# One fp32 transformer block on one core: the FFN's own DVE and ScalarE work entered in the scheduler's clock, six places for weight tiles in two sizes, and Wk loaded in four column chunks

## The chip, the cores and the metric

The kernel runs on one core of one Trainium2 chip. The metric is device time in microseconds, from a launch to its end. Before the change the median of three runs is 1770.16 us (1769.39 to 1774.62).

## What is computed

Everything is fp32: x is (4, 2048, 512), the context (4, 128, 512). Cut to what matters:

```python
# attention, per batch b: one head, 128 keys
xn = layernorm(x)
attn = softmax((xn @ Wq + bq) @ (ctx @ Wk + bk).T) / sqrt(512)
x1 = x + tanh(g_xattn) * (attn @ (ctx @ Wv + bv))
# FFN, one of 8 experts chosen per batch from the mean over the sequence
z = layernorm(x1)
e = argmax(z.mean(axis=1) @ Wr + br)
out = x1 + tanh(g_ffn) * (relu(z @ W1[e] + b1[e]) @ W2[e] + b2[e])   # 512 -> 2048 -> 512
```

## The kernel before

**The FFN** does nearly all the work. Per batch there are two pairs of blocks (a block is 512 rows) and two halves of the hidden width: 4 x 2 x 2 = 16 passes, called stage 0 to 15 below. Both layers are multiplied by Strassen's scheme in the Winograd form, which trades multiplications for sums. Layer 1 uses it twice, one inside the other: 7 groups (`ORDER`) of 7 products (`inner`), so 49 products of two matmuls. The matmuls of all products are recorded at one line, L798 (`chain`), with the names X, Y and Q for the PSUM banks; `z,w` are layer 1, `w,h` and `w,s` layer 2. The last three products of a group (5, 4, 3) run within the next group's. Layer 2 uses the scheme once: 7 products, each in two halves of eight matmuls (a pair below). ScalarE copies a bank to start the next (L817, L1032, L1043, L1064) and applies relu (L962); DVE and GpSimd do the sums (L978 to L1058, L1119, `hsum` L921).

**Weights.** The sums of weights that the scheme needs are made on the chip once per batch and half, mostly by GpSimd (`stage_half`): base blocks are loaded (L588, L594), summed (L559), and stored to a DRAM buffer, W1d or W2d (L580). Each pass then loads its tiles from there (L777, L771), or from W2 directly where no sum is needed (L764). `items` lists these loads in the order of use: for a group of layer 1 a left tile "A" (4 of 7 products, 4 KB per partition) and a right tile "B" (the last three, 3 KB in a place of 4 KB), for layer 2 seven tiles "2" (4 KB). `NW = 5` places take them in that order. After each group, and after each second half in layer 2, `fetch` issues as many loads as places have come free. The two loads of y, the running output of 1 MB each (L941, `sums_load`), are issued after group 5 in the first half of each pair, ahead of that group's `fetch`.

**Attention** for batch 0 runs ahead of the FFN. For batches 1 to 3 it runs inside the FFN: a generator per block (`attention`) that yields after each step what engines it used and for how long. Its steps: load x (L199, on ScalarE's queue) and xT (L201, on SP's), statistics on DVE (L208) and `pow` on GpSimd (L214), scores on TensorE (psc, L228) and DVE (L235), exp on ScalarE (L247), transposes (pp, L256), their copy (L259), the product with V (four pav, L282), which DVE adds into x (L270), statistics again, the store x1d (L293), normalising on ScalarE (L297), 16 transposes (pt, L329) that ScalarE copies back into x's buffer (L316), and the store z2d (L337) from there. pav and pt use two PSUM banks in turn, so a third waits until the first is read. There is one buffer for x, which the next block's load must wait for. The DMA semaphores are eight and used in turn, so every DMA also waits until the eighth before it in the program has landed.

**The order** is set in Python, as the program is written, by a clock that counts microseconds of TensorE: `tick` advances it after each product of layer 1 and each half of eight matmuls in layer 2. A stream (attention is `slow`, the weight sums are `staged`) may take its next step when the time `at` that its former steps have been given is at most `SOON` ahead of the clock, and when its pace allows: `PACE` times the clock's advance is the number of steps it may take. `free` holds when an engine is next free. Inside the FFN only GpSimd is kept there: steps on DVE and ScalarE add their time, times a factor of 1.3, to the stream's own `at`, and the FFN's own instructions add nothing but for a few on GpSimd (`pool_takes`). Each engine executes its own instructions strictly in the order written, and SP its DMAs.

**The set-up** loads the context of batch 0 (ctxT0), Wk in two column halves and Wq, makes keys (pk, L412) on TensorE, centres Wq on DVE (L463 to L465), and multiplies the two (pm, L412). ctxT0 and the keys KT0 lie in the two places of the pool `wk`, which the scores of attention use later.

Of the kernel before, what the change touches and what calls it, by code (L numbers as in the profile page):

```python
# [18 lines left out]
P = 128  # L19
# [70 lines left out]
def flamingo(tc, ctx, x, xT, cxT, g_x, g_f, WqT, Wk, Wv, bqk, bv, Wr, br, W1, b1, W2, b2, out):  # L90
# [4 lines left out]
    KC, FC = H // P, FF // P  # L95
    NW = 5
    TB = 4 * P
# [61 lines left out]

    zsum, Zs = {}, {}  # L160
    MV = {}
    done_at, clock = {}, {"now": 0.0}
# [30 lines left out]
    def attention(b, blk, pools):  # L193


        (xp, tag_x), (xTp, tag_xT), wk, ps_t, ps_a, queue = pools

        xt = xp.tile([P, 4, H], F32, tag=tag_x, name=f"x_{b}_{blk}")
        queue.dma_start(xt, rows(x, b, blk))  # L199
# [4 lines left out]
        def statistics():  # L204
            mv = small.tile([P, 4, 2], F32, tag="mv", name="mv", bufs=4)
            for t in range(4):
                st = small.tile([P, 6], F32, tag="st", name="st", bufs=4)
                nc.vector.bn_stats(st, xt[:, t, :])  # L208
                nc.vector.bn_aggr(mv[:, t, :], st)
                yield (("DVE", 0.85),)  # L210
            rstd = small.tile([P, 4], F32, tag="rstd", name="rstd", bufs=4)
            ve = small.tile([P, 4], F32, tag="ve", name="ve", bufs=4)
            nc.vector.tensor_scalar(ve, mv[:, :, 1], EPS, None, ALU.add)  # L213
            nc.gpsimd.tensor_tensor(rstd, ve, mhalf, ALU.pow)  # L214
            yield ("DVE", 0.15), ("POOL", 1.05), ("POW", 0.0 if ahead_of_ffn[0] else 1.0)
            return mv, rstd
# [29 lines left out]
        for t in range(4):  # L246
            nc.scalar.activation(  # L247
                sc[:, t, :], sc[:, t, :], AF.Exp,
                bias=nmax[:, t : t + 1], accum_out=ssum[:, t : t + 1],
            )  # L250
            if t % 2:
                yield (("ACT", 1.2),)
        yield from room(ps_t)
# [9 lines left out]
        nc.vector.tensor_scalar(coef, coef, gx, None, ALU.mult)  # L263
        yield (("ACT", 0.6),), (("DVE", 0.4),)
        while MV[b][1] is None:
# [76 lines left out]
    mvp = pool("mvp", 1)  # L342
    xp, xTp, wkp = pool("xp", 1), pool("xTp", 1), places("wk", 2)
    ps_t, ps_a = places("ps_t", 1, space=PSUM), places("ps_a", 1, space=PSUM)
# [17 lines left out]

    def in_home(p, tag, *shapes):

        t = p.tile([P, 4 * H], F32, tag=tag, name="home")
        at, out = 0, []
        for shape in shapes:
            n = int(np.prod(shape))
            v = t[:, at : at + n]
            names = "abcd"[: len(shape)]  # L370
            out.append(
                v.rearrange(
                    f"p ({' '.join(names)}) -> p {' '.join(names)}", **dict(zip(names, shape))
                ) if len(shape) > 1 else v
            )
            at += n
        return out

    if True:
        M0 = mvp.tile([P, KC, S], F32, tag="M", name="M_0")  # L380
        V0 = mvp.tile([P, H], F32, tag="V", name="V_0")
        ctxT0 = wkp.tile([P, 1, KC, S], F32, tag="wk", name="ctxT0")
        ctxTr = sp.tile([P, B - 1, KC, S], F32, name="ctxTr")
        w = {name: sp.tile([P, KC, H], F32, name=f"w{name}") for name in ("k", "q", "v")}
        bvb = sp.tile([P, H], F32, name="bvb")
        KT0 = wkp.tile([P, KC, S], F32, tag="wk", name="KT0")
        KTr, V3 = in_home(hp, "s2", (KC, (B - 1) * S), (H,))
# [6 lines left out]
        nc.sync.dma_start(ctxT0, cxT[:, 0:1])  # L394
        for c in range(2):
            nc.sync.dma_start(w["k"][:, :, c * Q : (c + 1) * Q], Wk[:, :, c * Q : (c + 1) * Q])
        with nc.allow_non_contiguous_dma(reason="bias"):
# [343 lines left out]
    items = [i for i in items if i[0] or i[1] == "2" or i[2] >= HERE]  # L741
    ring = {"issued": 0, "freed": 0}

    def ring_tile(kind):
        t = wp.tile([P, 4 * Q], F32, tag="w", name="w")
        if kind == "2":
            return t.rearrange("p (k c) -> p k c", k=4)
        k = 4 if kind == "A" else 3
        return t[:, 0 : 2 * k * P].rearrange("p (c k f) -> p c k f", c=2, k=k)

    def fetch(freed=0):

        ring["freed"] += freed
        while ring["issued"] < min(ring["freed"] + NW, len(items)):
            st, kind, i = items[ring["issued"]]
            b, fh = st // (2 * NF), st % 2
            need = (b, fh, "2" if kind == "2" else RIGHT[ORDER[i]])
            if need not in made and not (kind == "2" and RIGHT[ORDER2[i]] < 3):
                return
            t = ring_tile(kind)  # L760
            if kind == "2":
                m = ORDER2[i]
                if RIGHT[m] < 3:
                    nc.sync.dma_start(  # L764
                        t.rearrange("p (a k) c -> p a k c", a=2),
                        W2[bass.ds(expert[b][0], 1), fh, :, :, RIGHT[m]].rearrange(
                            "e a p k c -> p (e a) k c"
                        ),
                    )
# [38 lines left out]
    def inner(product, copied, begun, summed, done):  # L808
# [4 lines left out]
        def m1():  # L813
            t["X"] = bank("X")
            product(t["X"], 1, True)
            t["Y"] = bank("Y")
            nc.scalar.copy(t["Y"], t["X"])  # L817

        def m7():
# [27 lines left out]

    def pool_takes(us):
        free["POOL"] = max(free["POOL"], clock["now"]) + us

# [66 lines left out]
    def hsum(to, a, b, op, cp):  # L917

        for k in (slice(0, 2), slice(2, 4)):
            x, y, z = (t[:, cp, k, :] for t in (to, a, b))  # L920
            nc.vector.tensor_tensor(x, y, z, op)  # L921

    def s3(cp):
# [19 lines left out]
    def ffn1(b, blk, fh):  # L943
# [10 lines left out]
        def relu(ij, j, src):  # L954
# [6 lines left out]
            for c in range(2):  # L961
                nc.scalar.activation(  # L962
                    h[ij][:, v, 2 * m + c, :], src[:, c, :], AF.Relu,
                    bias=b1T[:, f + c : f + c + 1],
                )

        def ctile():
# [5 lines left out]
        def sums(m, j, v, eng):  # L973

            if m in BASE:
                ij, base = BASE[m]
# [17 lines left out]
        def group(i):  # L994
# [35 lines left out]
            def copied(v):  # L1030
                t = s7p.tile([P, 2, Q], F32, tag="s7", name="s7")
                nc.scalar.copy(t, v)  # L1032
                if m not in BASE:
                    return {21: t, 22: t}
# [3 lines left out]

            def begun(q, y):
                if m in BASE:  # L1040
                    nc.vector.tensor_tensor(q, BASE[m][1][21], y, ALU.add)
# [6 lines left out]

            def summed(j, a, v):
                if m == 1:  # L1050
                    nc.vector.tensor_tensor(first(j), a, v, ALU.add)
# [4 lines left out]
                else:  # L1056
                    c = cp_.tile([P, 2, Q], F32, tag="cg", name="cg", bufs=3)
                    nc.vector.tensor_tensor(c, a, v, ALU.add)  # L1058
                    sums(m, j, c, nc.gpsimd)
                    pool_takes(1.3)  # L1060

# [9 lines left out]
        for i in range(8):  # L1071
# [14 lines left out]
            left = 0 if s else HERE  # L1086
            fetch((cur is not None and i >= left) + (last is not None and i > left))
            if i == left:
# [5 lines left out]
    def ffn2(b, blk, fh, half):  # L1094
# [21 lines left out]
        def add(cp, j, v):  # L1116
            i, m = divmod(j - 11, 10)
            o = Ys[i][:, 2 * cp : 2 * cp + 2, m * Q : (m + 1) * Q]
            nc.vector.scalar_tensor_tensor(o, v, gf, o, ALU.mult, ALU.add)  # L1119

        def group(cp):
# [59 lines left out]

    BUSY = {"PE": 1.0, "DVE": 1.3, "ACT": 1.3, "POOL": 1.0, "DMA": 1.1, "Q": 1.1, "POW": 4.0}

    class Stream:
# [3 lines left out]
        def step(self):  # L1188
# [9 lines left out]
            elif chains:  # L1198
                ends = []
                for chain_ in (chains,) if isinstance(chains[0][0], str) else chains:  # L1200
                    t = self.at
                    for engine, us in chain_:
                        if engine == "POOL":
                            t = free[engine] = max(free[engine], t) + us
# [42 lines left out]
    while True:  # L1247
        s_ = min(parts, key=lambda s: s.at)
        if filler and max(filler.at, free["PE"]) + (SLACK if (0, NBLK - 1) not in done_at else PRESS) <= s_.at:
            if not filler.step():  # L1250
                filler = None
                setup.close()
                wp = pool("wp", NW, side="right")
            continue
# [44 lines left out]
    due = {"slow": 0.0, "staged": 0.0}  # L1299
    PACE = {"slow": (1.0,.9,.9), "staged": (3.,3.,3.,3.)}  # L1300
    next_stage = 1
    SOON = 0.8

    def paced(name, stream, more):

        due[name] = min(due[name] + more, 1.0 + more)
        while stream and due[name] >= 1 and stream.at <= clock["now"] + SOON:
            due[name] -= 1
# [4 lines left out]
    def tick(dt, weight):  # L1313
# [5 lines left out]
        for s_ in list(loose):  # L1319
            while s_.at <= clock["now"] + SOON:  # L1320
                if not s_.step():
# [8 lines left out]
    for b in range(B):  # L1330
        for blk in range(NF):
            for fh in range(2):
# [11 lines left out]
                for _ in ffn2(b, blk, fh, lambda: tick(1.73, 1.25)):  # L1344
                    for _ in range(3):
                        for name, us in next(prep, None) or ():
                            if name == "POOL":
                                pool_takes(us)
                    tick(1.73, 1.25)
# [33 lines left out]
```

## Time and profile before

| | |
|---|---|
| median of 3 runs | 1770.16 us |
| the profiled execution | 1770.84 us, span 1769.1 us |
| TensorE busy / weight loads | 1687.6 us (95%) / 1440.1 us (81%) |
| DVE, ScalarE, GpSimd busy | 1042.5, 581.4, 656.8 us |
| mean granted TensorE clock | 0.988 |
| DMA | 381.88 MB, 216 GB/s mean |
| FFN from, last matmul ends | 116 us, 1764.6 us |

The span goes from the first to the last instruction. Lines of groups read: line, engine, operation, what it writes and reads; waits read: who waited, for whom, us in total, times, longest. In a timeline a line is start, duration, and in brackets the idle time before it with the instruction that ended it; SPq and ACTq are the DMAs issued from SP and ScalarE. In the windows each line is a stretch with the busy time of each engine, the granted clock (1.00 is full speed), the DMA engines' busy share and GB/s.

### The profile page before, as it was taken

How to read it: one execution, taken by the hardware profiler on the slowest of the kernel's cores; microseconds unless marked ns; L12 is line 12 of the kernel's file. 1: busy time of each engine (PE TensorE's matmuls, PEld its weight loads, DVE VectorE, ACT ScalarE, POOL GpSimd, SP SyncE). 2: the span in 40 equal slices, each digit the busy share in tenths (PEclk: the TensorE clock that was granted, in tenths of full speed). 3: DMA queues.
4: the chain of work that ended last, by engine and by line, in shares of the span. 5: the costliest groups of instructions: out<-in, count | busy, mean ns of one | idle time of the engine just before them, and what ended most of it. 6: DMA issues, size and time to landing. Idle time of an engine off the chain costs nothing.

```text
span 1769.1 us, 21983 instructions
## 1 busy us (share of the span) xinstructions
PE 1687.6 (95%) x7966; PEld 1440.1 (81%) x7966; DVE 1042.5 (59%) x1663; ACT 581.4 (33%) x1284; POOL 656.8 (37%) x536
## 2 busy tenths in 40 slices
PE   6888988989999989899999999999999999999998
PEld 5667867877888878788887888888888888888887
DVE  5756837537578547566756666484546463656362
ACT  1514224143241432424334152332324141415150
POOL 0464513410069541244614940168644410251010
PEclk9999999999999999999999999999999999999999
DMA  7277767373678784638787693487767452535241
GB/s 292 96 265 301 256 236 249 104 265 104 217 276 331 266 335 163 228 119 299 263 301 246 252 353 139 153 290 245 250 246 282 140 185 87 184 125 200 78 142 70
DMA packets 142012, 381.88 MB, mean 216 GB/s; under 512 B 10448, under 2 KB 39120, under 8 KB 127568
## 3 DMA queue, kind: packets, MB, share of 16 engines
q1 hardware_dynamic: 135856, 342.43, 55.5%
q10 hardware_dynamic: 6048, 38.04, 5.5%
q8 instruction: 64, 1.05, 0.2%
q14 instruction: 44, 0.36, 0.1%
HBM read 262.99 MB, written 117.44 MB: 215 GB/s over the span
## 4 chain that ended last, share of the span: by engine, by line
PE 81%; DMA 8%; DVE 6%; POOL 2%; ACT 2%; issue 1%; SPq 0%; ACTq 0%; DVEq 0%; POOLq 0%
PE Y L798 32%; PE Q L798 21%; PE X L798 20%; PE psc L228 3%; DMA w<-W1d 2%; PE pav L282 2%; DMA z2d<-x 2%; DVE st L208 1%; DMA W1d<-base 1%; PE pt L329 1%; DMA w<-in_W_dram 1%; POOL home L559 1%; DMA base<-in_W_dram 1%; DVE x L270 1%; DVE c L990 1%
## 5 line engine op out<-in xcount | busy, mean ns | idle before, releaser
L798 PE MATMUL Y<-z,w 128*128 128x256 f32 x1296 | 325.0, 384 | 23.8 <-DMA w<-W1d 6.6
L798 PEld LDWEIGHTS Y<-z,w 128*128 128x128 f32 x1296 | 243.4, 191 | 73.4 <-issue 11.3
L962 ACT ACTIVATE h<-c,b1T 128x256 f32<-128x256 f32 x512 | 229.1, 501 | 91.0 <-DVE c L978 33.5
L559 POOL TENSOR_TENSOR base<-base 128x512 f32<-128x512 f32 (+1 forms) x126 | 184.1, 1466 | 199.5 <-DMA base<-in_W_dram 189.0
L817 ACT COPY Y<-X 128x512 f32<-128x512 f32 x144 | 82.1, 571 | 468.5 <-PE X L798 444.7
L798 PE MATMUL X<-w,h 128*128 128x256 f32 x1024 | 231.1, 382 | 5.2 <-DMA w<-in_W_dram 5.2
L798 PE MATMUL Q<-w,h 128*128 128x256 f32 x1024 | 229.9, 381 | 4.0 <-DMA w<-W2d 3.7
L798 PE MATMUL Y<-w,h 128*128 128x256 f32 x1024 | 228.0, 379 | 0.0
L798 PEld LDWEIGHTS X<-w,h 128*128 128x128 f32 x1024 | 195.7, 192 | 33.1 <-issue 6.5
L798 PEld LDWEIGHTS Q<-w,h 128*128 128x128 f32 x1024 | 195.2, 191 | 33.5 <-issue 6.4
L798 PE MATMUL X<-z,w 128*128 128x256 f32 x864 | 210.4, 382 | 7.9 <-DMA w<-W1d 7.9
L798 PEld LDWEIGHTS Y<-w,h 128*128 128x128 f32 x1024 | 193.9, 190 | 27.7 <-issue 1.9
L798 PE MATMUL Q<-z,w 128*128 128x256 f32 x864 | 210.2, 382 | 1.0 <-DVE r L992 0.7
L798 PEld LDWEIGHTS X<-z,w 128*128 128x128 f32 x864 | 164.6, 192 | 33.5 <-issue 5.8
L798 PEld LDWEIGHTS Q<-z,w 128*128 128x128 f32 x864 | 164.3, 192 | 28.0 <-issue 3.8
L981 POOL TENSOR_TENSOR r<-r,cg 128x512 f32<-128x512 f32 x32 | 40.7, 1270 | 344.1 <-DVE cg L1058 331.9
L559 POOL TENSOR_TENSOR z<-z 128x256 f32<-128x256 f32 x156 | 132.0, 869 | 43.2 <-DVE z L559 39.5
L214 POOL TENSOR_TENSOR rstd<-ve,mhalf 128x4 f32<-128x4 f32 x32 | 35.2, 1100 | 294.3 <-DVE ve L213 294.1
L798 PE MATMUL Y<-w,s 128*128 128x256 f32 x512 | 113.8, 379 | 0.0
L208 DVE BATCH_NORM_STATS2 st<-x 128x6 f32<-128x512 f32 x128 | 86.9, 679 | 40.8 <-DMA x<-in_x_dram 40.8
L798 PEld LDWEIGHTS Y<-w,s 128*128 128x128 f32 x512 | 97.1, 190 | 14.4 <-issue 1.4
L1119 DVE SCALAR_TENSOR_TENSOR y<-Y,gf,y 128x512 f32<-128x512 f32 x64 | 47.9, 749 | 99.0 <-PE Y L798 96.2
(150 smaller groups left out, 2009.0 us busy)
## 6 DMA issues: line engine op xcount, KB each, us to landing
w<-W1d SPq DMA_DIRECT2D x108, 512.0 KB, 4.3
w<-W1d SPq DMA_DIRECT2D x108, 384.0 KB, 3.5
w<-W2d SPq DMA_DIRECT2D x64, 512.0 KB, 5.4
base<-in_W_dram SPq DMA_DIRECT2D x29, 1024.0 KB, 8.9
W1d<-base SPq DMA_DIRECT2D x14, 1792.0 KB, 9.7
w<-in_W_dram SPq DMA_DIRECT2D x48, 512.0 KB, 5.3
W1d<-tt SPq DMA_DIRECT2D x14, 1344.0 KB, 7.0
xT<-in_xT_dram SPq DMA_DIRECT2D x16, 1024.0 KB, 10.7
```

The lines of the kernel that those rows point to most:

```text
L208: nc.vector.bn_stats(st, xt[:, t, :])
L214: nc.gpsimd.tensor_tensor(rstd, ve, mhalf, ALU.pow)
L228: nc.tensor.matmul(psc[:, t, :], lhsT=xTt[:, kc, t * P : (t + 1) * P], rhs=Mb[:, kc, :], start=kc == 0, stop=kc == KC - 1,)
L270: nc.vector.scalar_tensor_tensor(xt[:, t, :], t_, coef[:, t : t + 1], xt[:, t, :], ALU.mult, ALU.add)
L282: nc.tensor.matmul(pav[t][0], lhsT=pT[:, t * P : (t + 1) * P], rhs=Vb, start=True, stop=True)
L329: nc.tensor.transpose(pt[kc][0][:, t * P : (t + 1) * P], z[:, t, kc * P : (kc + 1) * P], ident)
L559: eng.tensor_tensor(o, l, r, ALU.subtract)
L798: nc.tensor.matmul(bank[:, c, :], lhsT=left(k, c), rhs=right(k, c), start=fresh and c == 0 and k == 0, stop=c == 1 and k == ks - 1, skip_g ...
L817: nc.scalar.copy(t["Y"], t["X"])
L962: nc.scalar.activation(h[ij][:, v, 2 * m + c, :], src[:, c, :], AF.Relu, bias=b1T[:, f + c : f + c + 1],)
L981: eng.tensor_tensor(r[j], r[j], v, ALU.add)
L1119: nc.vector.scalar_tensor_tensor(o, v, gf, o, ALU.mult, ALU.add)
```

## The change

1. The places for weight tiles become four of 4 KB (tiles "A" and "2") and two of 3 KB (tiles "B"), each with a count of its own. The order of the loads stays: a load whose kind has no free place holds back those behind it.
2. `pool_takes` becomes `takes`, for any engine. Copies, relu, sums and `hsum` of the FFN enter their time in `free` for DVE and ScalarE, and streams' steps on these engines queue there too.
3. An attention block in the FFN pauses for 9 us (times 1.1) before its loads. After `pow` the pause of 4 us (1.0 times the factor of POW) becomes one of `SOON`; pauses of `SOON` and 0.8 `SOON` are put behind the last exp and the copy of the transposes.
4. `SOON` goes from 0.8 to 1.4, the pace of attention from (1.0, .9, .9) to (3, 1.2, 1.2).
5. Wk is loaded by four chunks of 128 columns. The pool `wk` has one place instead of two; ctxT0 and KT0 lie in the buffer `tt`, which the first weight sums use later.

```diff
-    NW = 5
+    NW = {"A": 4, "B": 2}
...
+        if not ahead_of_ffn[0]:
+            yield (("DMA", 9),)
         xt = xp.tile([P, 4, H], F32, tag=tag_x, name=f"x_{b}_{blk}")
...
-            yield ("DVE", 0.15), ("POOL", 1.05), ("POW", 0.0 if ahead_of_ffn[0] else 1.0)
+            yield ("DVE", 0.15), ("POOL", 1.05), ("GAP", 0.0 if ahead_of_ffn[0] else SOON[0])
...
             if t % 2:
-                yield (("ACT", 1.2),)
+                yield ("ACT", 1.2), ("GAP", SOON[0] * (t // 2) * (not ahead_of_ffn[0]))
...
-        yield (("ACT", 0.6),), (("DVE", 0.4),)
+        yield (("ACT", 0.6), ("GAP", SOON[0] * 0.8 * (not ahead_of_ffn[0]))), (("DVE", 0.4),)
...
-    xp, xTp, wkp = pool("xp", 1), pool("xTp", 1), places("wk", 2)
+    xp, xTp, wkp = pool("xp", 1), pool("xTp", 1), places("wk", 1)
...
-        ctxT0 = wkp.tile([P, 1, KC, S], F32, tag="wk", name="ctxT0")
+        ctxT0, KT0 = in_home(stp, "tt", (1, KC, S), (KC, S), n=21 * P)
...
-        KT0 = wkp.tile([P, KC, S], F32, tag="wk", name="KT0")
...
-        for c in range(2):
-            nc.sync.dma_start(w["k"][:, :, c * Q : (c + 1) * Q], Wk[:, :, c * Q : (c + 1) * Q])
+        for c in range(KC):
+            nc.sync.dma_start(w["k"][:, :, c * P : (c + 1) * P], Wk[:, :, c * P : (c + 1) * P])
...
-    ring = {"issued": 0, "freed": 0}
+    ring = {"issued": 0, "A": NW["A"], "B": NW["B"]}
     def ring_tile(kind):
-        t = wp.tile([P, 4 * Q], F32, tag="w", name="w")
+        if kind == "B":
+            t = wp.tile([P, 3 * Q], F32, tag="wb", name="w", bufs=NW["B"])
+        else:
+            t = wp.tile([P, 4 * Q], F32, tag="w", name="w", bufs=NW["A"])
...
-    def fetch(freed=0):
-        ring["freed"] += freed
-        while ring["issued"] < min(ring["freed"] + NW, len(items)):
+    def fetch(a=0, b=0):
+        ring["A"] += a
+        ring["B"] += b
+        while ring["issued"] < len(items):
             st, kind, i = items[ring["issued"]]
+            place = "B" if kind == "B" else "A"
+            if not ring[place]:
+                return
...
             t = ring_tile(kind)
+            ring[place] -= 1
...
-    def pool_takes(us):
-        free["POOL"] = max(free["POOL"], clock["now"]) + us
+    def takes(engine, us, behind=1.0):
+        free[engine] = max(free[engine], clock["now"] + behind) + us
...
             nc.vector.tensor_tensor(x, y, z, op)
+            takes("DVE", 0.65)
...
                     bias=b1T[:, f + c : f + c + 1],
                 )
+            takes("ACT", 1.0)
...
+            if eng is nc.vector or m == 5:
+                takes("DVE", 0.7 * (1 + (m == 5 and eng is nc.vector)))
...
             def summed(j, a, v):
+                takes("DVE", 0.7)
...
-                    pool_takes(1.3)
+                    takes("POOL", 1.3, 2.0)
...
-            fetch((cur is not None and i >= left) + (last is not None and i > left))
+            fetch(cur is not None and i >= left, last is not None and i > left)
...
-                        if engine == "POOL":
+                        if engine in ("DVE", "ACT", "POOL"):
                             t = free[engine] = max(free[engine], t) + us
...
-    PACE = {"slow": (1.0,.9,.9), "staged": (3.,3.,3.,3.)}
+    PACE = {"slow": (3.,1.2,1.2), "staged": (3.,3.,3.,3.)}
-    SOON = 0.8
+    SOON = [1.4]
...
-                            if name == "POOL":
-                                pool_takes(us)
+                            if name in ("POOL", "DVE"):
+                                takes(name, us, 0.0)
```

More of the change, by code (lines that the diff above doesn't have):

```diff
@@ L361, in flamingo, with in_home @@
     sp = pool("setup", 1, setup, side="right")
-    def in_home(p, tag, *shapes):
-        t = p.tile([P, 4 * H], F32, tag=tag, name="home")
+    def in_home(p, tag, *shapes, n=4 * H):
+        t = p.tile([P, n], F32, tag=tag, name="home")
         at, out = 0, []
@@ L817, in m1 @@
             nc.scalar.copy(t["Y"], t["X"])
+            takes("ACT", 0.6)
         def m7():
@@ L1032, in copied @@
                 nc.scalar.copy(t, v)
+                takes("ACT", 0.6)
+                takes("DVE", 0.7 * (m in BASE))
                 if m not in BASE:
@@ L1039, in begun @@
             def begun(q, y):
+                takes("DVE" if m in BASE else "ACT", 0.65)
                 if m in BASE:
@@ L1119, in add @@
             nc.vector.scalar_tensor_tensor(o, v, gf, o, ALU.mult, ALU.add)
+            takes("DVE", 0.75)
         def group(cp):
@@ L1179, in flamingo @@
     ctx.enter_context(tc.manual_schedule())
-    BUSY = {"PE": 1.0, "DVE": 1.3, "ACT": 1.3, "POOL": 1.0, "DMA": 1.1, "Q": 1.1, "POW": 4.0}
+    BUSY = {"PE": 1.0, "DVE": 1.3, "ACT": 1.3, "POOL": 1.0, "DMA": 1.1, "Q": 1.1, "POW": 4.0, "GAP": 1.0}
     class Stream:
@@ L1252, in flamingo @@
                 setup.close()
-                wp = pool("wp", NW, side="right")
+                wp = pool("wp", 1, side="right")
             continue
@@ L1299, in flamingo @@
     due = {"slow": 0.0, "staged": 0.0}
-    PACE = {"slow": (1.0,.9,.9), "staged": (3.,3.,3.,3.)}
+    PACE = {"slow": (3.,1.2,1.2), "staged": (3.,3.,3.,3.)}
     next_stage = 1
-    SOON = 0.8
     def paced(name, stream, more):
         due[name] = min(due[name] + more, 1.0 + more)
-        while stream and due[name] >= 1 and stream.at <= clock["now"] + SOON:
+        while stream and due[name] >= 1 and stream.at <= clock["now"] + SOON[0]:
             due[name] -= 1
@@ L1319, in tick @@
         for s_ in list(loose):
-            while s_.at <= clock["now"] + SOON:
+            while s_.at <= clock["now"] + SOON[0]:
                 if not s_.step():
```

## The prediction

> **What bounds the kernel now.** I read the page, then TensorE's waits, then the timelines around its longest waits, then the windows for the clock.
>
> ```profile
> span 1769.1 us, 21983 instructions
> PE 1687.6 (95%) x7966; PEld 1440.1 (81%) x7966; DVE 1042.5 (59%) x1663; ACT 581.4 (33%) x1284; POOL 656.8 (37%) x536
> PE 81%; DMA 8%; DVE 6%; POOL 2%; ACT 2%; issue 1%; SPq 0%; ACTq 0%; DVEq 0%; POOLq 0%
> ```
>
> TensorE is the bound. The change alters the count of no compute instruction on any engine (in the order of the two built programs only Wk's loads go from two to four), so what it can win is the 81.5 us in which TensorE is not busy (1769.1 - 1687.6) and the time in which its clock is lowered. Of the 81.5 us some 21 lie in the set-up before 116 us and 4.5 after the last matmul (1757.67 + 6.92 against 1769.1); some 53 lie in the FFN, before 1340 us. The list of TensorE's waits names them:
>
> ```profile
> PE X L798 <- DMA w<-W1d: 7.9, 2, 5.1
> PE Y L798 <- DMA w<-W1d: 6.6, 4, 2.4
> PE Y L798 <- ACT Y L817: 6.3, 2, 3.5
> PE Y L798 <- ACT Q L1043: 6.1, 1, 6.1
> PE X L798 <- DMA w<-in_W_dram: 5.2, 1, 5.2
> PE pav L282 <- ACT sc L259: 5.0, 8, 1.1
> PE Y L798 <- DVE Q L1041: 4.8, 4, 2.2
> PE Q L798 <- DMA w<-W2d: 3.7, 1, 3.7
> ```
>
> Few, long and each with a cause of its own. The longest, in the timelines of ScalarE and TensorE:
>
> ```profile
> 382.50 0.33 ACTq L337 DMA_DIRECT2D z2d<-x  x1
> 392.95 0.34 ACTq L199 DMA_DIRECT2D x<-in_x_dram  x1
> 393.33 0.59 ACT L1032 COPY s<-Q 128x512 f32<-128x512 f32 x1 [10.32 <-DMA z2d<-x]
> 394.57 2.07 PE L798 MATMUL Y<-z,w 128*128 128x256 f32 x4 [6.13 <-ACT Q L1043]
> ```
>
> The next block's load of x stands in ScalarE's queue right behind the store that must first leave that buffer. ScalarE stands 10.3 us, and TensorE, which runs on for some 4 us, stands 6.13. Then four matmuls take 2.07 us, where elsewhere they take 1.13: the clock has dropped. The windows show it (fourth from the end is the granted clock): 0.14 x 25 = 3.5 us lost here, nothing late in the kernel.
>
> ```profile
> 375.00:400.00 25.00, 18.87 (x85) 16.04 (x84) 8.67 (x13) 8.14 (x20) 6.86 (x5) 0.86 0.82 305
> 1450.00:1475.00 25.00, 25.00 (x117) 22.02 (x116) 9.14 (x13) 2.88 (x5) 0.00 (x0) 1.00 0.28 85
> ```
>
> In the same way 225-250 and 625-650 lose 3.5 us each, 125-150, 300-325 and 725-750 1.75 each.
>
> A page's rule stands against part of this: the Trainium skill, "TensorE: Matmul & The Clock Gate", section "HAM oscillation", counts only idle gaps above about 3.4 us as dangerous. Here the clock also dropped behind a gap of 2.76 us (728.22, eight matmuls in 3.13 us, 1.89 elsewhere), so by the rule term 1 below would be 1.75 us smaller, and I go by the row.
>
> **The change part by part.** I write stage 0 to 15 for the FFN's passes (batch, pair of blocks, half). Layer 1 has groups 0 to 6 of seven products of 0.86 us (a group is 6.05 us; its last three products run within the next), layer 2 seven pairs of 6.91 us (the chain's "x32" rows).
>
> 1. The pause before an attention block's loads (9 x 1.1 = 9.9 us in the model). In the built order the load of x now stands 10 or 11 products (8.6 to 9.5 us) behind the z2d store in layer 1, at least 1.25 pairs (8.6 us) behind it in layer 2, instead of 0 to 1 place. The store takes 8.2 us from issue to landing (median row), and ScalarE has some 3 us of slack (it stood 10.3, TensorE 6.1). What goes: 6.13 (394.57), 2.76 (728.22), 0.38 (1070.40), 1.77 behind the second (739.18 and 742.57), and 3.5 + 1.75 of clock, 16.3 in all. I keep 3 for late stores: **-13**, between -16 and 0. The queue that follows is ScalarE's alone; the xT load on SP moves with it. Next late there: the x load also waits for the eighth DMA before it (that is how the DMA semaphores rotate), mostly tile loads of 4 to 5 us.
>
> 2. The first x load in the FFN moves from before group 1 to group 2 of stage 0. Before, it held ScalarE until 126.07 and TensorE 3.55 us; then TensorE waited 2.81 more for W1d tiles landing at 146.4, and 1.75 of clock. Now it waits for the last Vd store, issued at 128.36 with 9.3 us to landing: ScalarE would stand from 127 to 137.7, less 3 of slack, which is 8 us. But the weights come at about the same time as before (their loads now go ahead of xT's 1 MB). Bounds -8 and +4; I take **0**, since the landing of the weights ends the wait in both.
>
> 3. Stage 1's first weights (5.13 us at 234.70, 3.5 of clock). They are made by GpSimd and stored at 219.68, landing in 10.89. In the new order the second half's base load comes 0.25 pairs (1.7 us) and the store 0.5 pairs (3.5 us) sooner, and a block's 16 score matmuls (3.57 us) stand in front of the waiting product. Bounds -8.6 and +1 (GpSimd's chain unmoved, TensorE merely earlier at the wait): **-4**. Then W2d: its first tiles for stage 1 are asked for after group 6 rather than one pair into layer 2, where they were needed at once: 3.66 + 1.75, **-5** (0 if GpSimd is late).
>
> 4. Stage 4's direct W2 tile. Before:
>
> ```profile
> 611.77 0.35 SPq L594 DMA_DIRECT2D base<-in_W_dram  x1
> 612.17 1.84 SPq L941 DMA_DIRECT2D y<-x1d  x2
> 614.79 0.39 SPq L764 DMA_DIRECT2D w<-in_W_dram  x1
> 631.05 6.51 PE L798 MATMUL X<-w,h 128*128 128x256 f32 x16 [5.18 <-DMA w<-in_W_dram]
> ```
>
> 16 us for one tile, among a base load of 1 MB, 2 MB of y and another base load at 617.19. With attention paced faster at the start (3 against 1.0) routing ends earlier, and both base loads now stand in groups 1 and 2. 5.18 + 0.82 (617.30) + 3.5 of clock go, 1.5 stays: **-8**, between -9.5 and 0.
>
> 5. The gaps put behind rstd, exp and the copy of the transposed scores. TensorE waited in the FFN 3.9 us for that copy (five pav) and 1.7 for exp (two pp): **-4**, bounds -5.6 and 0. The DVE's own FFN work in the clock: waits for DVE of some 6.7 us not counted above (2.23 at 948.75 the longest). Now steps are held while the model's DVE is busy, but let go 1.4 us ahead instead of 0.8. Bounds -6 and +6: **-2**.
>
> 6. Right tiles behind stores of W1d. 2.18, 1.21 and 2.36 us (1034.04, 1237.60, 1337.93), each a 3-KB tile with a store of 1.8 MB just ahead in SP's queue. A 3-KB tile is now issued one product (0.86 us) sooner, as it no longer waits for the group's last product. The stores of stage 8 and 11 move away, but in stage 6 and 10 one stands directly ahead of such a tile, in 7 and 9 some half group ahead: 3 us stay, **-3**, bounds -5.75 and +2.
>
> 7. What the six places add. Five 4-KB places ran in one order, so the last right tile was asked for after group 4. With two 3-KB places it must wait until group 5 frees one, and in the eight stages with y loads it is queued behind those 2 MB. It is needed one group and one product later, 6.9 us. The nearest row is the tile that stood at this place before, in stage 14 (issued 1615.48):
>
> ```profile
> y<-x1d SPq DMA_DIRECT2D x2, 1024.0 KB, 8.8
> w<-in_W_dram SPq DMA_DIRECT2D x1, 512.0 KB, 6.8
> ```
>
> 6.8 us with 512 KB, so 384 KB just arrive. Where a further 1 MB lies ahead (stages 0, 4, 6, 10), at the 390 GB/s seen there, 2.6 us more. I take 1.2 us in each of four, **+5**; bounds 0 (all land) and 8 x 2.4 = +19. In layer 2 four tiles are ahead instead of five, three pairs (20.7 us) against a 5.4 us load: nothing. In return the third left tile is already there when a stage begins.
>
> 8. Denser attention. With faster pace and 1.4 us ahead, eight of twelve blocks have 12 or 16 of their transposes in one place, and eight have three or four pav in one place. A third transpose in one place waited 0.34 us (204.30, 459.74), a third pav 0.39 to 1.31 for the sum on DVE. Twelve blocks x 0.4 to 0.5 over before: **+5**, bounds 0 and +14.
>
> 9. Wk in four. The first pk waited 7.52 us for half of Wk, but pm waits for Wq centred on DVE, which begins at 13.83, and Wq, issued at 4.78, lands at 13.1 (8.3): at most 0.7 us to win. The two further loads put Wq's issue behind gf's landing (1.18 + 4.5) instead of gx's (0.74 + 4.0): 0.9 late, and x and xT some 1.4. **0**, bounds -0.7 and +1.5. The single wk place and the home of ctxT0 and KT0 cost nothing: their next users are seconds of work behind in the same order (the fourth block's scores, the first outer sums), and attention blocks in the FFN follow one another; if they did not, a block's scores would wait some 4 us for pav.
>
> Weighing Wk by a page: the Trainium skill, "DMA: Bandwidth & Descriptors", section "Bandwidth", lists 0.95 us for 64 KB and 6.15 for 1 MB (another issuing path), an estimate of 2 us for a quarter of Wk and thus a start some 2 us sooner; the trace's 256-KB load (ctxT) took 3.8 us.
>
> Sum: -13 + 0 - 4 - 5 - 8 - 4 - 2 - 3 + 5 + 5 + 0 = -29 us. The profiled execution took 1770.84 us (span 1769.1 and 1.7 around it), 0.7 above the median of 1770.16. 1770.8 - 29 is 1741.8; against the median **1742 us**.
>
> **The rivals.** (A) The gains are half eaten: the stalls of terms 1 and 4 go, but production at the start is bound by GpSimd's chain (terms 3 at +1 and 0, 9 us less) and the denser blocks cost +11 instead of +5: 1742 + 10 + 6 = 1758. For it: the chain of waits shows base load, sums, store and tile load end to end from 162.80 to 234.70. Against it: loads and stores in that chain do stand earlier. (B) Slower: the last right tile (term 7). Without it the sum is -34. It decides from 34 / 8 = 4.3 us per stage with y loads, clock included. At 5 us and 1.75 of clock in eight stages it is +54 - 34, about 1790. For it: y's loads took 8.8 us and several MB are then in flight. Against it: the 6.8 us row at the very place. (C) The pacing does nothing: waits reappear at other places, as the x load merely waits for another DMA; terms 1 and 4 at half, 3, 5 and 6 at zero: -10.5 + 10, no change, 1770.
>
> **How the numbers follow.** Forecast 0.62 (1728 to 1752); A 0.19 (1752 to 1765); better than 1728, terms 2, 3 and 7 at their good ends, 0.07; C 0.05; B 0.07. From 1726 to 1766 some 0.82 lies. A run of this kernel can be told from no change beyond about 0.3% (5.3 us): faster 0.87, same 0.05, slower 0.08.
>
> **What would show it.** Right: no wait of ScalarE for z2d above 3 us in layer 1; no TensorE wait above 3 us between 240 and 1340 us, and the clock at 1.00 in those windows; the in_W tile of stage 4 gone from the list. Wrong: TensorE waits on W1d tiles at the last product group of even stages (term 7), pt and pav waits summing above 12 us (8), a wait at 230-235 us unchanged (3).

## The result and the profile after

The changed kernel takes **1741.14 us** (median of 6 runs, 1735.92 to 1743.12) against 1768.85 for the kernel before in the same comparison: a ratio of 0.984, 95% interval 0.982 to 0.986. The profiled execution took 1742.86 us in all, with a span of 1741.1, that is 28.0 less than the span before. The forecast was 1742.

The page of the changed kernel: span, busy times, and the shares of the chain of waits.

```profile
span 1741.1 us, 21919 instructions
...
PE 1686.3 (97%) x7965; PEld 1439.3 (83%) x7966; DVE 1048.7 (60%) x1663; ACT 581.9 (33%) x1284; POOL 654.6 (38%) x536
...
PE 86%; DVE 6%; DMA 4%; issue 1%; ACT 1%; POOL 1%; SPq 0%; DVEq 0%; POOLq 0%; ACTq 0%
```

TensorE's busy time is 1.3 us less; its idle time went from 81.5 to 54.8 (1741.1 - 1686.3). So the gain is idle time, and the DMA's share of the chain is halved. TensorE's waits of the changed kernel (us in total, times, longest):

```profile
PE Y L811 <- DMA w<-W1d: 8.8, 5, 3.6
PE Y L811 <- DVE Q L1063: 7.4, 7, 2.8
PE pm L417 <- DVE wq L470: 7.2, 4, 3.7
PE pk L417 <- DMA wk<-in_Wk_dram: 6.4, 1, 6.4
PE pav L288 <- DVE x L276: 4.6, 3, 3.1
PE pt L335 <- ACT x L322: 3.4, 9, 0.5
PE pv L450 <- ACT Ms L438: 2.9, 1, 2.9
PE begin L1302 <- DVE home L455: 2.8, 1, 2.8
```

The rows of before for ScalarE's copies (6.3 and 6.1), for W1d at a stage's start (7.9), for the direct W2 tile (5.2) and for W2d (3.7) are gone. Four of the rows that are left belong to the set-up. For the FFN alone I added all TensorE waits above 0.25 us by what ended them, and the clock's loss by windows of 25 us ((1 - granted) x 25, an upper bound, as a low clock costs nothing while TensorE is idle):

| FFN, us | before | after |
|---|---|---|
| weight tiles (DMA) | 23.4 | 8.8 |
| ScalarE's copies of X and Y | 12.4 | 0 |
| exp, copy of the transposed scores | 5.6 | 0 |
| DVE, attention included | 11.9 | 12.0 |
| transposes (pt) | 0.7 | 2.9 |
| all waits | 53.9 | 23.7 |
| clock's loss, at most | 15.8 | 7.5 |
| first X product to last matmul | 1648.3 | 1613.8 |

The FFN became 34.5 us shorter and the whole kernel 28.0, because the FFN begins later, at 123.03 instead of 116.34. That was not foreseen.

The place that the prediction showed first, in windows (fourth from the end is the granted clock):

```profile
375.00:400.00 25.00, 24.24 (x112) 19.00 (x111) 18.05 (x34) 13.62 (x35) 3.49 (x2) 1.00 0.55 199
725.00:750.00 25.00, 24.66 (x127) 21.71 (x126) 17.85 (x26) 7.63 (x16) 17.73 (x21) 1.00 0.54 198
```

Both had lost clock before (0.86 and 0.93) and are now full. ScalarE waits nowhere for a z2d store any more; before, it did so six times, for 56.5 us.

### The profile page after: what moved, and what is told of

It reads as the page before. It is cut to its first block, busy times and chain, and to the rows that moved or that the text cites. A ratio compares the mean times of both kernels' runs of the same rounds, so it can differ in the third digit from the quotient of the medians.

```text
span 1741.1 us, 21919 instructions
## 1 busy us (share of the span) xinstructions
PE 1686.3 (97%) x7965; PEld 1439.3 (83%) x7966; DVE 1048.7 (60%) x1663; ACT 581.9 (33%) x1284; POOL 654.6 (38%) x536
## 4 chain that ended last, share of the span: by engine, by line
PE 86%; DVE 6%; DMA 4%; issue 1%; ACT 1%; POOL 1%; SPq 0%; DVEq 0%; POOLq 0%; ACTq 0%
PE Y L811 34%; PE Q L811 23%; PE X L811 21%; DMA w<-W1d 3%; PE pav L288 2%; PE psc L234 2%; PE pt L335 1%; DVE st L214 1%; DMA home<-in_W_dram 1%; PE pm L417 1%; PE pv L450 1%; DVE x L276 1%; DVE c L1009 1%; PE pk L417 0%; DMA wq<-in_WqT_dram 0%
## 5 line engine op out<-in xcount | busy, mean ns | idle before, releaser
L1142 DVE SCALAR_TENSOR_TENSOR y<-X,gf,y 128x512 f32<-128x512 f32 x32 | 23.9, 746 | 135.3 <-issue 70.7
```

## The experiments

Twelve kernels, in three sets, each timed beside the kernel before (1767.8, 1768.4 and 1768.9 us). The table is the map; what each showed follows.

| kernel | us | 95% interval of the ratio to before |
|---|---|---|
| before + pause | 1989.1 | 1.122 to 1.128 |
| before + pause + pace | 1777.1 | 1.002 to 1.006 |
| after - pause | 1821.3 | 1.029 to 1.032 |
| after - pause - places | 1806.7 | 1.018 to 1.024 |
| after - spacing | 1807.7 | 1.020 to 1.024 |
| after - spacing - clock entries | 1789.5 | 1.010 to 1.013 |
| after - clock entries | 1750.6 | 0.987 to 0.993 |
| after - places | 1743.5 | 0.985 to 0.988 |
| after, Wk in halves | 1742.2 | 0.983 to 0.987 |
| after, y loads late | 1742.9 | 0.983 to 0.988 |
| after, Wk in halves and y late | 1743.0 | 0.984 to 0.989 |
| after, pace 1.5 | 1756.1 | 0.990 to 0.995 |

### The pause alone, and the change without it

```
  before:  + if not ahead_of_ffn[0]:
           +     yield (("DMA", 9),)
             xt = xp.tile(...)          # attention, ahead of the loads
  after:   the same two lines removed
```

> The kernel before with the pause of 9 us ahead of an attention block's loads and nothing else of the change. Theory (term 1, ScalarE's queue stands on the load of x behind the store z2d): ScalarE's waits on z2d, 56.5 us in six before, fall below 8 us; TensorE's waits at about 394, 728 and 127 us go, with their clock, which is 16 + 5 us; the time falls by 12 to 22 us. Rival (it is the pacing and the places for tiles that bring the gain, and the pause only moves the stall to another DMA): less than 6 us. Attention then ends two stages later than before (in stage 11), so the weight sums of batches 2 and 3 start later, which can give some of it back.

> The changed kernel without the pause of 9 us ahead of an attention block's loads, all else kept. Theory: the load of x stands directly behind z2d again in nine of eleven blocks, four or five of them in layer 1; ScalarE waits there 8 to 11 us each, TensorE 3 to 6 us and its clock drops: 12 to 30 us slower than the changed kernel, so 1753 to 1771. Rival (pacing and the clock model bring the gain): within 6 us of the changed kernel.

The pause alone in the old kernel: **1989 us**, 221 slower, where a gain was expected. ScalarE's waits for z2d did go. What came instead, from TensorE's waits and then from its timeline:

```profile
PE X L800 <- DMA w<-W1d: 185.9, 6, 47.3
PE X L800 <- issue: 42.0, 1, 42.0
```

```profile
605.52 2.07 PE L800 MATMUL X<-z,w 128*128 128x256 f32 x4 [43.44 <-DMA w<-W1d]
```

(The profile names no releaser for the second row, one idle time ahead of stage 8.) And from SyncE's queue at that place:

```profile
580.43 0.51 SPq L582 DMA_DIRECT2D W1d<-base  x1
583.69 0.35 SPq L596 DMA_DIRECT2D base<-in_W_dram  x1
596.94 0.33 SPq L582 DMA_DIRECT2D W2d<-base  x1
597.47 0.34 SPq L546 DMA_DIRECT2D b2g<-in_b_dram  x1
597.92 3.84 SPq L779 DMA_DIRECT2D w<-W1d  x5
```

The first tiles of stage 4 stand in SyncE's queue behind a store that waits for GpSimd's sums, and these wait for a base load that was issued late. They are late because the router is: its copy of the z sums (zb<-zm on DVE) lies at 498.5, 988.2 and 1479.4 us for the second to fourth sample, against 465.4, 802.3 and 1137.9 before. So at the old pace the attention stream has no room for twelve pauses of 9.9 us; the kernel with the new pace, below, tests that.

The other way round, the changed kernel without its pause takes **1821 us**, 80 more than with it, where 1753 to 1771 was expected. ScalarE's waits for z2d are back (58 us), but the largest TensorE wait is another, in stage 2. SyncE's queue and TensorE there:

```profile
394.81 0.52 SPq L787 DMA_DIRECT2D w<-W1d  x1
404.06 0.36 SPq L539 DMA_DIRECT2D b1T<-in_b_dram  x1
...
405.48 0.36 SPq L204 DMA_DIRECT2D xT<-in_xT_dram  x1
406.02 0.58 SPq L590 DMA_DIRECT2D base<-in_W_dram  x1
406.71 1.12 SPq L954 DMA_DIRECT2D y<-x1d  x2
407.93 0.41 SPq L787 DMA_DIRECT2D w<-W1d  x1
...
422.41 2.05 PE L808 MATMUL Y<-z,w 128*128 128x256 f32 x4 [11.32 <-DMA w<-W1d]
```

SyncE issues nothing from 395.3 to 404.06. The first load then is b1T, which needs the router's answer, and the router's zb copy lies at 398.2. SyncE's own waits in the trace show what it stood for: 7.9 us for `ei`, the router's choice of expert. Then xT, base and y lie ahead of the right tile, which TensorE waits for 11.3 us. So here the other parts without the pause make the kernel slower than before, as the pause does without them. The changed kernel with the old pace was not tried.

### The pause with the pace

```
  before + pause, and
  - PACE = {"slow": (1.0,.9,.9), ...}
  + PACE = {"slow": (3.,1.2,1.2), ...}
```

> The kernel before with the pause of 9 us and the new pace (3, 1.2, 1.2), without the clock model, the other pauses, the six places and the four chunks of Wk. Theory: pause and pace belong together (the pause alone starves the weight sums: TensorE waited 23 to 47 us at the start of six stages); together they give most of the gain, since ScalarE's 56.5 us on z2d and the in_W tile of stage 4 go: 1740 to 1755. Rival (the pauses behind rstd, exp and the transposes' copy, with DVE's work in the clock, carry half of it): 1757 or more, with waits for DVE and ScalarE above 15 us in the FFN.

1777 us: the starving is cured (212 us back), and yet it is 8 us slower than before. The theory (1740 to 1755) missed, and the rival (1757 or more) held. TensorE's waits of this kernel:

```profile
PE Y L800 <- DMA w<-W1d: 16.2, 3, 9.7
PE pt L331 <- ACT x L318: 8.9, 10, 2.3
PE X L800 <- DMA w<-in_W_dram: 8.4, 3, 5.8
...
PE pav L284 <- ACT sc L261: 6.7, 13, 0.7
...
PE X L800 <- DMA w<-W1d: 4.0, 2, 3.5
PE pp L258 <- ACT sc L249: 2.8, 3, 1.4
```

Against the changed kernel that is some 20 us more of weight tiles (16.2 + 8.4 + 4.0 against 8.8), 5.5 more of pt, 5.6 of pav, 2.8 of pp: 34 us. From its first X product to the last matmul the FFN is 46 us longer here (1659.9 against 1613.8). The clock's loss is at most 17.0 against 7.5, up to 9.5 of the remaining 12. The medians are only 36 apart, since the FFN begins at 116.08 here and at 123.03 after. The router lies at 430.2, 788.8 and 1134.0, against 418.9, 740.8 and 1075.1 after.

### The spacing and the clock's entries

"Spacing" is the gaps behind rstd, exp and the copy, and SOON. With the old ones a step follows rstd by 4.0 us in the model instead of 1.4, nothing is spaced behind exp and the copy, and steps are let go 0.8 us ahead instead of 1.4. The gaps and SOON were changed together and not tried apart. The kernels without the clock's entries also lose the 2 us that the changed kernel adds ahead of one of GpSimd's entries (`behind`).

```
  - SOON = [1.4]                      + SOON = [0.8]
  - ("GAP", SOON[0])    # rstd        + ("POW", 1.0)   # x 4.0
  - ("GAP", ...)        # exp, copy   (removed)

  clock entries out: takes() does nothing for DVE and ACT, and
  - if engine in ("DVE", "ACT", "POOL"):
  + if engine == "POOL" or ahead_of_ffn[0] and engine in free:
```

> The changed kernel with DVE and ScalarE out of the clock model again (their FFN work enters no time, and streams' steps on them do not queue), with the pause, the other pauses, pace, SOON and places kept. Theory (term 5: worth 2 us, between -6 and +6): 1738 to 1748, waits for DVE up by 2 to 6 us. Rival (the clock model is the change's core): 1755 or more.

> The kernel after with the spacing of the attention steps as before (4 us behind rstd instead of 1.4, none behind exp and behind the copy of the transposed scores, steps let go 0.8 us ahead instead of 1.4); pause, pace, entries in the clock, places and Wk as after. The pause with the pace alone came to 1777, after is 1741, and after without the DVE's and ScalarE's entries in the clock 1750.6, without the places 1743.5. Theory (the spacing carries what these two leave, some 36 - 9 - 2 = 25 us, and it shows as TensorE's waits for ScalarE at pp, pav and pt and as weights that come late): 1758 to 1770. Rival (spacing and clock model cover for one another, so either alone is enough): 1742 to 1752.

> The same without the DVE's and ScalarE's entries in the clock as well: this is before plus the pause, the pace, the six places and Wk in four. Theory (places and Wk do next to nothing, as after without either showed): 1772 to 1780, as the pause with the pace alone (1777). Rival (with this order the places matter, since there TensorE waited 20 us for W1d tiles and 8 us for W2 tiles, against 9 and 0 in after): 1750 to 1766.

Without the entries: 1750.6, 9 us slower, between the two expectations. Without the spacing: **1807.7, 67 us slower**, beyond both. Without both: 1789.5, so here taking the entries away *gains* 18 us, where with the new spacing it costs 9. Expected was 1772 to 1780 or less. The kernel without the spacing: TensorE's longest row of waits, its timeline, and SyncE's queue:

```profile
PE X L811 <- DMA w<-W1d: 57.2, 4, 33.2
```

```profile
603.34 2.04 PE L811 MATMUL X<-z,w 128*128 128x256 f32 x4 [33.19 <-DMA w<-W1d]
```

```profile
577.92 0.56 SPq L585 DMA_DIRECT2D W1d<-base  x1
581.12 0.36 SPq L599 DMA_DIRECT2D base<-in_W_dram  x1
594.78 0.33 SPq L585 DMA_DIRECT2D W2d<-base  x1
595.31 0.34 SPq L549 DMA_DIRECT2D b2g<-in_b_dram  x1
595.78 4.28 SPq L790 DMA_DIRECT2D w<-W1d  x6
```

It is the picture of the pause alone, at the same place: the tiles stand behind the W2d store, that behind GpSimd, and GpSimd waits for a base load (16.48 us at 530.50, 11.59 at 589.48). The router tells how far each kernel's attention has come:

| router's zb copy, us | sample 2 | 3 | 4 | time |
|---|---|---|---|---|
| after - clock entries | 395.0 | 699.3 | 998.1 | 1750.6 |
| after - pause | 398.2 | 724.7 | 1018.0 | 1821.3 |
| after | 418.9 | 740.8 | 1075.1 | 1741.1 |
| after, pace 1.5 | 419.8 | 746.0 | 1079.2 | 1756.1 |
| before + pause + pace | 430.2 | 788.8 | 1134.0 | 1777.1 |
| after - spacing - clock entries | 438.9 | 796.9 | 1139.1 | 1789.5 |
| before | 465.4 | 802.3 | 1137.9 | 1768.9 |
| after - spacing | 472.0 | 910.3 | 1286.0 | 1807.7 |
| before + pause | 498.5 | 988.2 | 1479.4 | 1989.1 |

Pause and clock entries hold the attention stream back; pace and spacing (the 2.6 us less behind rstd, the further reach ahead) let it go. Where the last column has 1286 and 1479 instead of 1075, the time is 67 and 248 us longer: by the program the weights of the next sample hang on the router. Earlier than after gains nothing in the two kernels that show it; without the pause SyncE stands for the router and the loads behind it collide. The router's time is not all: before is at 465.4 and "after - spacing" at 472.0, but there a base load issued at 504.44 in the one leaves at 520.76 in the other.

### The places, y's loads, Wk, and a faster pace

```
  five places:  one tag, NW = 5, tiles in one order, as in the kernel before
  y late:       sums_load(b, blk) after fetch(...) instead of ahead of it
  Wk in halves: for c in range(2): dma_start(w["k"][:, :, c*Q:(c+1)*Q], ...)
  pace 1.5:     "slow": (3.,1.5,1.5)
```

> The changed kernel with five 4-KB places in one order again, all else kept. Theory (term 7: the six places cost about what they bring): the last right tile is asked for after group 4 again, so the wait at 176.6 us (3.57 us, W1d tile in stage 0) goes or shrinks; the third left tile of a stage comes one group later, which nothing waits for. -5 to +3 us against the changed kernel. Rival (the sixth place is what keeps W1d tiles in time): waits on W1d tiles grow from 8.8 us to above 15 and the time rises by more than 8 us.

> The changed kernel with the two loads of y issued behind the tile loads of group 5 instead of ahead. If the 2 MB of y ahead of the last right tile make the wait at 176.6 us (3.57 us and some 1.7 of clock), it goes: -3 to -6 us. Rival: SP stands on the store of W2d until GpSimd's sums end (issued at 165.48, y at 165.91, the tile at 167.35), and the tile is late whatever stands between: less than 2 us, the wait still above 2 us.

> The changed kernel without the pause and with five 4-KB places in one order. Without the pause alone TensorE waited 42.5 us for W1d tiles in 8 waits, up to 11.3. Theory (term 7 at its bad end: the last right tile, asked for one group later and behind y, x and xT loads, is what is late): these waits fall below 20 us and the time by more than 15 us against 1821, to 1785 to 1805. Rival (the transfers are too dense whatever the places): above 1813, W1d waits above 30 us.

> The changed kernel with Wk in two halves. Theory (term 9): pk starts at 7.4 instead of 6.4 us, pm no later (15.4 against 15.5), no difference in the time beyond 1.5 us. The FFN began at 116.3 us before and at 117.6 to 123.0 in four kernels with the four chunks, behind a drop of the clock near 95 us and a wait for V of 0.4 to 3.1 us: if the four chunks cause that, it begins at 116 to 117 here and the time falls by some 4 us; if it is the clock's phase, anywhere between 116 and 123.

> The kernel after with Wk in two halves and y's loads behind the last right tile. With Wk in halves the FFN began 6.7 us sooner in the profiled execution (116.3 against 123.0) and lost as much to the first W1d tiles (4.1) and to sums of DVE; y late took the wait of 3.6 us for the last right tile of stage 0 away and others came. Theory (stage 0 is bound by its weight sums and loads, whatever TensorE does before): 1738 to 1745, the same as after. Rival (the two add up, 3 to 8 us): 1732 to 1737.

> The kernel after with the attention stream paced at (3, 1.5, 1.5) instead of (3, 1.2, 1.2). The pause with the old pace (1, 0.9, 0.9) starved the weight sums by 220 us; this asks whether 1.2 is still short of it. Theory (nothing is starved any more, no TensorE wait above 3 us has the pace as its cause, and denser attention costs a few us of waits for exp, the copies and the sums): 1740 to 1752. Rival (the weights' sums still come late with 1.2): 1730 to 1738.

*Places.* Five instead of six: 1743.5 against 1741.1, with overlapping runs. The W1d waits are 7.6 at Y and 2.1 at X, and in place of the wait at 176.6 us stands one of 2.6 for a direct W2 tile. So the six places give nothing that can be told here. Without the pause five are better by 15 us (1806.7 against 1821.3), just above what the theory had (1785 to 1805): W1d tiles still take 27.3 us and direct W2 tiles 13.8. And the kernel with the old spacing, no entries, six places and Wk in four is 12 slower than the one with five and Wk in halves (1789.5 against 1777.1; 2.6 of it lie before the FFN, 118.67 against 116.08). In neither pair of kernels is the split ring a help.

*y late.* The 3.57 us wait of stage 0 goes, as expected, and nothing is won (1742.9): DVE's Q takes 4.48 at 166.03, and a sum 3.26 at 183.62.

*Wk in halves.* The same time (1742.2), but the FFN begins at 116.32, not at 123.03. Stage 0's waits in this kernel:

```profile
134.81 0.70 PE L811 MATMUL Y<-z,tt 128*128 128x256 f32 x2 [1.81 <-ACT Q L1065]
144.40 1.25 PE L811 MATMUL X<-z,w 128*128 128x256 f32 x4 [4.14 <-DMA w<-W1d]
164.98 1.40 PE L811 MATMUL Y<-z,w 128*128 128x256 f32 x4 [2.13 <-DVE Q L1063]
176.09 2.05 PE L811 MATMUL Y<-z,w 128*128 128x256 f32 x4 [3.87 <-DMA w<-W1d]
```

The first two, 5.95 us, are not there after: stage 0 is bound by its first made weights, and 6.7 us won ahead of them are waited away. The two together (Wk in halves, y late) give 1743.0, as the theory had it (1738 to 1745); no kernel here beats the change.

*Pace 1.5.* 15 us slower, beyond both expectations (1740 to 1752, 1730 to 1738). pt waits 10.8 us (two of 2.65 and 3.01), W1d tiles 16.2, two of them at 608.07 and 836.93 with more than 4 us and a clock that drops; the router is no earlier than with 1.2. So faster pace only packs the steps, and 1.2 is enough.

## Why the prediction was right

The number was right (1742, measured 1741.1) and the likeliest case held. By its terms, with the waits that went and came; the second figure of a span takes in the clock's loss by windows, its upper bound:

| term | forecast | measured |
|---|---|---|
| 1 pause | -13 | -11 to -16 |
| 2 first x load | 0 | -6 to -8 |
| 3 stage 1's W1d, W2d | -9 | -9 to -14 |
| 4 direct W2 tile | -8 | -6 to -9.5 |
| 5 exp and copy; DVE | -4; -2 | -5.6; +1.4 to +4.9 |
| 6 tiles behind stores | -3 | -0.5 |
| 7 last right tile | +5 | +3.6 to +5.3 |
| 8 denser attention | +5 | +3 to +5 |
| 9 Wk in four | 0 | +6.7 at the FFN's start (+1.3 to +6.7 over nine kernels) |

The measured column adds up to some -23 by the waits alone and some -32 with the clock's loss at its bound; the spans differ by 28.0. Terms 1, 3, 4, 7, 8 and the first half of 5 came about as they were read. The mechanism held, but that the sum came within 1 us is partly luck: term 6 and term 5's half on DVE came out some 6 us dearer, others cheaper, without a common cause. That half had its sign wrong, inside its bounds of -6 and +6: the waits that it counted, 6.7 us, became 8.2. (Two readings in the prediction are off and change no sum: by its own figures ScalarE's slack is 4.2 us, not 3, and rival A takes 10 us from term 3, not 9.)

**Terms 9 and 2 missed, and cancel for one reason.** Term 9 was bounded at +1.5 and measured +6.7: its working went by Wq, and did not follow the set-up to its end. There TensorE ran at a lower clock (0.84 against 0.93 from 75 to 100 us), and DVE's sums ahead of the first product took longer. TensorE in the set-up, before and then after:

```profile
94.61 1.03 PE L516 MATMUL pr<-wr,zb 128*128 128x8 f32 x8 [2.09 <-issue]
95.50 3.70 PE L412 MATMUL pk<-ctxTr,wk 128*128 128x256 f32 x16
```

```profile
95.28 1.85 PE L521 MATMUL pr<-wr,zb 128*128 128x8 f32 x8 [2.14 <-DVE zb L515]
96.98 6.17 PE L417 MATMUL pk<-ctxTr,wk 128*128 128x256 f32 x16
```

and DVE, before and then after:

```profile
111.30 0.69 DVE L450 TENSOR_TENSOR V<-pv,bvb 128x512 f32<-128x512 f32 x1 [0.39 <-PE pv L445]
111.91 2.88 DVE L559 TENSOR_TENSOR tt<-base,tt 128x896 f32<-128x896 f32 x2
```

```profile
115.26 0.69 DVE L455 TENSOR_TENSOR V<-pv,bvb 128x512 f32<-128x512 f32 x1 [2.87 <-PE pv L450]
115.86 5.38 DVE L564 TENSOR_TENSOR tt<-base,tt 128x896 f32<-128x896 f32 x2
```

The eight small pr matmuls took 1.85 instead of 1.03 us and the sixteen pk behind them 6.17 instead of 3.70: 3.3 us by the clock; the two sums 2.5 more. The cause is Wk's four loads by this: in all nine profiles with four the FFN begins between 117.60 and 123.03, in all five with two between 116.08 and 116.93. What was profiled here is the far end of that: the median of the nine is 118.91, 2.6 later than before.

The traces also tell most of why the amounts differ. In five of the nine the granted clock from 95 to 100 us is 0.52 to 0.66 and the sixteen pk take 5.39 to 6.17 us; in the other four, and in all five with two loads, it is 1.00 and they take 3.70. In six of the nine (these five and the kernel with y late) the two DVE sums are slow as well, 3.96 to 5.66 us together: there at least one of them begins behind GpSimd's first sum of 128x896 (see the last section). In the three with neither, the FFN begins at 117.60 to 117.75, 1.3 to 1.4 late and inside the bound of +1.5. What stays open is how four loads at the start bring the clock's drop at 95 us.

Term 2 said that the landing of the first weights ends the wait wherever the x load stands, and so 0. The kernel with Wk in halves bears it out: with the FFN beginning at 116.3 again, stage 0 waits 1.81 + 4.14 there, against 3.55 + 2.81 before. In the three profiles whose FFN begins at 118.67 to 119.03, the wait for these tiles is 2.0 to 2.1 us. What the changed kernel shows as a gain of term 2 is the late start, which lies in front of the same wait. So the one term that came out beyond its bounds is 9, and it cost nothing, because a wait that ends at a fixed time stood behind it.

Term 6 was over-sized: 5.3 us of waits stay of 5.8 (2.12 at 789.45 and 1.92 at 907.49 the longest), and the kernel with five places has 7.6. Term 7 showed in stage 0 alone, and not by the 2 MB of y only:

```profile
165.48 0.33 SPq L585 DMA_DIRECT2D W2d<-home  x1
165.91 1.35 SPq L957 DMA_DIRECT2D y<-x1d  x2
167.35 0.91 SPq L790 DMA_DIRECT2D w<-W1d  x1
```

```profile
176.59 1.57 PE L811 MATMUL Y<-z,w 128*128 128x256 f32 x4 [3.57 <-DMA w<-W1d]
```

y and the tile stood in SyncE's queue behind a W2d store that waited 11.0 us for GpSimd. The other seven such stages wait nothing for this tile, stages 4, 6 and 10 among them, where 1.2 us each had been put. With y moved behind the tile the wait went and the time did not. Of the signs that were named, one failed: a TensorE wait above 3 us is left between 240 and 1340 (3.15 at 968.78, for a sum on DVE), and the windows from 800 and 950 have a clock of 0.93.

**What the sum does not tell** is what each part is worth. Term 1 gave the pause 13 us, read off waits that it removes; alone it costs 221 us, and to take it from the changed kernel costs 80. The spacing, priced at -4 with the clock's entries at -2, costs 67 to take away, the entries 9. The terms are right for the change as a whole, whose built order was read. They do not hold for its parts, for each of which another order would be built.

The rivals: (A), half eaten, put GpSimd's chain as the bound of stage 1; its wait went. (B), the last right tile, needed 4.3 us per stage and found them at most in one of eight. (C), waits that reappear elsewhere, did not come for the whole change, but it is what six of the incomplete versions showed, those slower than before, and then beyond the gain.

The page on TensorE's clock that the prediction weighed (the Trainium skill, "TensorE: Matmul & The Clock Gate", section "HAM oscillation") counts gaps above about 3.4 us. The set-up rows above agree less with it still: behind a wait of 2.14 us the pr matmuls took 1.8 times as long. In four other profiles (waits of 1.72, 2.13, 2.14 and 2.15 us) pr took 1.03, but the clock dropped in the pk right behind it, 5.39 to 5.41 us instead of 3.70. In the remaining nine, with waits of 2.08 to 2.13, it did not drop. So neither 3.4 us nor any length alone tells here whether the clock drops.

## What to carry to other kernels

When a planner builds the order, cost a change on the order that it builds as a whole; a part of it that is taken out makes another order, and here, of the parts that gave 28 us together, the pause and the spacing cost 80 and 67 us when missing, the clock's entries 9, and the places and Wk's chunks nothing that can be told. Where a wait is moved into a paced stream, look at who stands last behind that stream (here the router, and through it the next weights) and give the stream back the time that the wait takes. Time won or lost ahead of a wait that ends at a fixed time was worth nothing here: look for that wait before you price the work in front of it.

## What the runs showed of the hardware

In the fourteen profiles TensorE stands idle for 1.72 to 2.15 us at the same place in the set-up. Behind that the granted clock fell in five of them (0.52 to 0.66 from 95 to 100 us) and stayed at 1.00 in nine; a wait of 2.13 us is among both.

The same two DVE sums (128x896, float32) took 2.74 to 5.66 us together in the fourteen profiles. GpSimd runs a group of sums beside them in all, first of 128x256, then of 128x896; the first of 128x896 begins at 113.14 to 116.82 us, 115.45 before and 115.34 after. The 20 of these DVE sums that began ahead of it took 1.07 to 1.50 us each, the 8 that began behind it 2.50 to 2.85. Before, the two began at 111.91 and 113.29; after, at 115.86 and 118.40. So it is not the overlap by itself: the time goes with which of GpSimd's sums is already running. Why is not shown here.
